# The last token group of a two-layer transformer kernel: first experts in two halves, and an unread TensorE product behind each piece

## The chip, the cores and the metric

The kernel runs on one core of a Trainium2 chip. The metric is the device time of one execution in microseconds (us); less is better. Five engines matter here: TensorE (PE in the profile, its weight loads PEld), VectorE (DVE), ScalarE (ACT), GpSimd (POOL) and SyncE (SP, which here issues the plain DMAs). Each engine takes its instructions from its own queue, strictly in order, and waits at an instruction until what it needs has been signalled.

## The reference: what is computed

One sequence of T = 2048 tokens of C = 128 features goes through two layers. Cut to what matters:

```python
x = x + attn0(layernorm(x))     # 16 heads of 64, softmax over all 2048 keys, and x again as residual
x = x + ffn0(layernorm(x))      # 16 experts; a token's weights are non-zero for 4 of them, out of 2 of 4 groups
x = x + attn1(layernorm(x))     # 8 heads; each token sees 64 local keys and 32 chosen ones
x = x + ffn1(layernorm(x))      # a shared expert of 256, and 2 of 8 experts fixed by the token's number
# attn1: I = sum_h iw[h] * relu(q_i[h] @ k_i.T); own 64 keys first, future ones out; top 96 by I
```

`attn1` needs, for every token, an index score against every earlier token, the 32 best of them, and their rows of keys and values.

## The kernel before, in words

**Tiles and groups.** Tokens lie in 16 tiles of 128 (one token to a partition) and 4 groups of 4 tiles. The main loop in `run` (L422) does layer 0's attention for all groups. Beside it, `advance` takes pieces of the later stages of a group whose attention is finished: `follow(g)` (L588) chains three Python generators, `experts0` (L599), `attention1` (L725) and `experts1` (L1055), and each `yield` hands back an estimated cost. When the attention ends, the last group (tiles 12 to 15) is left and nothing runs beside it: L502 to L505 close the attention's pools, set `self.alone` and run through `follow(3)`. I call this stretch the tail.

**The order of the work.** The code is traced in program order; a scheduler then puts each engine's instructions in an order by that priority and by its own model of when operands are ready. At run time each engine follows that list. An instruction passed to `keep_in_program_order` is pinned behind everything traced before it on its engine. In the tail a product takes its PSUM bank by `x()` (L138) from a cycle through all eight banks, `all_banks` (L120).

**`experts0`.** Layer norm (`layernorm`, L66), transposes (`transposed`, L145), then gating: a product `pg`, a sigmoid and comparisons that rank groups and experts (`below`, L637), weights `we`, and their transpose `ptw`. Every token goes through all 16 experts, with weight zero where it isn't routed. `hidden` (L710) is two products `p1b` and `p3b` of 512 columns (4 tiles of tokens) on PE, Tanh and Identity on ACT (L718, L719) and two DVE operations (L721, L722); then four products `py` (L702) and four DVE operations of 128x128 (L705) add the result to the residual `xr`. In the tail `ahead` = 4 experts' `hidden` are issued ahead. The weights `wb` come by SP, 192 KB an expert.

**`attention1`.** First, for 4 tiles together, layer norm and the products of keys and index queries (`pk`, `pm`, `ptk`: L733 to L781; I call it prepare), with a table of key rows written to DRAM. Then, tile by tile:
- `index_scores(n)` (L792): products `pi` (L802), Relu on ACT (L807), and DVE sums into the scores `v` (L804, L808), 64 + 128n wide, here 1600 to 1984.
- `choose(n)` (L824): four rounds of MAX8, FIND_INDEX8 and MATCH_REPLACE8 over `v` on DVE (L835, L837, L840), a transpose of the indices `ixT` (L842), and 32 indirect gathers of key rows into `kv` on POOL (L853), pinned in program order.
- `queries(n)` (L866): `pq`, softplus on ACT (L86 to L88: Abs, Exp, Ln), a rotation on DVE (L97 to L104), transposes `ptq` (L905).
- `attend(n)` (L913): rotation of the gathered rows on DVE (pinned), transposes `ptr`, scores `pl` (L942 adds a mask by a bf16 product of `identb` with `smask`, 416 columns), maxima and Exp (L962, L966), transposes `pte` (L983), `po`, and sixteen products `pj` (L1012) added to `xr` (L1013).

`beside(k, first, other)` takes k pieces of `other` behind each piece of `first`. The tail's order (L1031 to L1042) is: index 12, choose 12, index 13, choose 13; index 14 beside queries 12, choose 14 beside attend 12; the same with 15 and 13; then queries 14, attend 14, queries 15, attend 15. `experts1` follows.

Of the kernel before, what the change touches and what calls it, by code (L numbers as in the profile page):

```python
# [8 lines left out]
F32 = mybir.dt.float32  # L9
# [8 lines left out]
P = 128  # L18
# [88 lines left out]
class Program:  # L107
# [3 lines left out]
    def __init__(self, ctx, tc, a, out):  # L111
        self.ctx, self.tc, self.nc, self.a, self.out = ctx, tc, tc.nc, a, out
        nc = self.nc
        self.cp = ctx.enter_context(tc.tile_pool(name="const", bufs=1))
        self.dp = ctx.enter_context(tc.tile_pool(name="dram", bufs=1, space=DRAM))
        self.ps_s = ctx.enter_context(tc.tile_pool(name="ps", bufs=5, space=PSUM))
        self.ps_o = ctx.enter_context(tc.tile_pool(name="po", bufs=1, space=PSUM))
        self.ps_x = ctx.enter_context(tc.tile_pool(name="px", bufs=2, space=PSUM))
        s, o, x = (self.ps_s, "ps"), (self.ps_o, "po"), (self.ps_x, "x")
        self.all_banks = itertools.cycle((s, x, s, o, s, x, s, s))  # L120
        self.alone = False
# [22 lines left out]

    def transposed(self, src, dst, name):  # L145

        pt = self.x(name)
        for j in range(4):
            self.nc.tensor.transpose(pt[:, j, :], src[:, j, :], self.ident)
        self.nc.scalar.copy(dst, pt.rearrange("p a b -> p (a b)"))  # L150
# [271 lines left out]
    def run(self):  # L422
# [81 lines left out]
        for _ in self.follow(3):  # L504
            pass  # L505
# [82 lines left out]
    def follow(self, g):  # L588

        for stage in (self.experts0, self.attention1, self.experts1):  # L590
            with ExitStack() as sc:
                yield from stage(sc, g)
# [6 lines left out]
    def experts0(self, sc, g):  # L599
        nc, w, xr = self.nc, self.w, self.xr[g]  # L600
        sm = sc.enter_context(self.tc.tile_pool(name="b_sm", bufs=1, side="right"))

        ahead = 4 if self.alone else 0
        hp = sc.enter_context(self.tc.tile_pool(name="b_h", bufs=2 + ahead, side="right"))
        wp = sc.enter_context(self.tc.tile_pool(name="b_w", bufs=4 + ahead, side="right"))
        wx = [self.weights(wp, e, f"wb{g}_{e}") for e in range(2 + ahead)]
        xn = sm.tile([P, 4, C], F32, tag="xn", name=f"xn1_{g}")
        layernorm(nc, sm, xr, xn, "ln1")
        yield 5.0
        xT = sm.tile([P, 512], F32, tag="xT", name=f"xT1_{g}")  # L610
# [14 lines left out]
        pg = self.x(f"pg{g}", [P, 4, NE0])  # L625
        for j in range(4):
            nc.tensor.matmul(pg[:, j, :], xT[:, j * P : j * P + P], w["wg"], start=True, stop=True)
        s = sm.tile([P, 4, NE0], F32, tag="s", name=f"gs{g}")
# [8 lines left out]
        def below(v, n, first, k, tag):  # L637

            shape = [P, 4, n, n]
# [4 lines left out]
            ff = bcast(first.rearrange("p a b -> p (a b)"), 1, 4)  # L644
# [3 lines left out]
            rank = sm.tile([P, 4, n], F32, tag="rank" + tag, name=f"rank{tag}{g}")  # L648
# [4 lines left out]
        gm = sm.tile([P, 4, NG0], F32, tag="gm", name=f"gm{g}")  # L653
# [4 lines left out]
        goff = sm.tile([P, 4, NG0], F32, tag="goff", name=f"goff{g}")  # L658
        nc.vector.tensor_scalar(goff, gsel, 1.0, None, ALU.subtract)
        ms = sm.tile([P, 4, NE0], F32, tag="ms", name=f"ms{g}")  # L660
# [7 lines left out]
        we = sm.tile([P, 4, 32], F32, tag="we", name=f"we{g}")  # L668
        wh = sm.tile([P, 4, NE0], F32, tag="wh", name=f"wh{g}")
        nc.vector.memset(we, 0.0)  # L670
        nc.vector.tensor_tensor(we[:, :, 0:NE0], s, esel, ALU.mult)
        ws = sm.tile([P, 4], F32, tag="ws", name=f"ws{g}")
        wr = sm.tile([P, 4], F32, tag="wr", name=f"wr{g}")
# [6 lines left out]

        pt = self.x(f"ptw{g}", [P, P])
        nc.tensor.transpose(pt, we.rearrange("p a b -> p (a b)"), self.ident)
        wt = sm.tile([P, P], F32, tag="wt", name=f"wt{g}")
        nc.scalar.copy(wt, pt)
        yield 1.0
        pb = self.x(f"pb2_{g}")
        nc.tensor.matmul(pb.rearrange("p a b -> p (a b)"), wt, w["b2"], start=True, stop=True)
# [4 lines left out]
        for e in range(NE0 + 1):  # L692
            if e + ahead < NE0:
                if e + ahead + 2 < NE0:
                    wx.append(self.weights(wp, e + ahead + 2, f"wb{g}_{e + ahead + 2}"))
                hidden(e + ahead)
                yield 2.0
            if e > 0:
                h = hs.pop(e - 1)
                py = self.x(f"py{g}_{e}")  # L700
                for j in range(4):
                    nc.tensor.matmul(py[:, j, :], h[:, j * P : j * P + P], wx[e - 1][:, 2, :], start=True, stop=True)  # L702
                yield 1.0
                for j in range(4):
                    nc.vector.scalar_tensor_tensor(  # L705
                        xr[:, j, :], py[:, j, :], wh[:, j, e - 1 : e], xr[:, j, :], ALU.mult, ALU.add
                    )
                yield 1.0

    def hidden(self, pool, wx, xT, b1, hb1, b3, name):  # L710

        nc = self.nc
        p1, p3 = self.x("p1" + name, [P, 512]), self.x("p3" + name, [P, 512])
        nc.tensor.matmul(p1, wx[:, 0, :], xT, start=True, stop=True)  # L714
        nc.tensor.matmul(p3, wx[:, 1, :], xT, start=True, stop=True)  # L715
        th = pool.tile([P, 512], F32, tag="th", name="th" + name)
        z = pool.tile([P, 512], F32, tag="z", name="z" + name)
        nc.scalar.activation(th, p1, AF.Tanh, scale=0.5, bias=hb1)  # L718
        nc.scalar.activation(z, p1, AF.Identity, bias=b1)  # L719
        h = pool.tile([P, 512], F32, tag="h", name="h" + name)  # L720
        nc.vector.scalar_tensor_tensor(h, th, 1.0, z, ALU.add, ALU.mult)  # L721
        nc.vector.scalar_tensor_tensor(h, p3, b3, h, ALU.add, ALU.mult)  # L722
        return h

    def attention1(self, sc, g):  # L725
# [7 lines left out]
        cols = slice(512 * g, 512 * g + 512)  # L733
# [4 lines left out]
        with ExitStack() as prep:  # L738
            pp = prep.enter_context(tc.tile_pool(name="c_prep", bufs=1, side="right"))
            xn = pp.tile([P, 4, C], F32, tag="xn", name=f"xn2_{g}")  # L740
            layernorm(nc, pp, xr, xn, "ln2")
            yield 5.0
            xT = pp.tile([P, 512], F32, tag="xT", name=f"xT2_{g}")
            self.transposed(xn, xT, f"pt2_{g}")
# [3 lines left out]
            pk = self.x(f"pk{g}", [P, 4, 64])  # L748
            for j in range(4):
                nc.tensor.matmul(pk[:, j, :], xT[:, j * P : j * P + P], w["wck"], start=True, stop=True)  # L750
            kg = pp.tile([P, 4, 64], F32, tag="kg", name=f"kg{g}")
            nc.scalar.copy(kg[:, :, 0:32], pk[:, :, 0:32])
            softplus(nc, pp, kg[:, :, 32:64], pk[:, :, 32:64], self.one, "spk")
            nc.sync.dma_start(table.rearrange("(n p) d -> p n d", p=P)[:, 4 * g : 4 * g + 4, :], kg)
            yield 3.0
            for i, (dst, wt) in enumerate(
                ((kiT[:, cols], w["iwk"]), (qiT[0], w["iwq"][:, 0:128]), (qiT[1], w["iwq"][:, 128:256]), (cqT, w["wdq1"]))
            ):
                m = 64 if i == 3 else P
                pm = self.x(f"pm1_{g}_{i}", [P, 512])  # L760
# [7 lines left out]
            kl = pp.tile([P, 4, 2, 64], F32, tag="kl", name=f"kl{g}")  # L768
# [4 lines left out]
                cs[:, 0, 4 * g : 4 * g + 4, :], cs[:, 1, 4 * g : 4 * g + 4, :], "rk",  # L773
# [3 lines left out]
            pt = self.x(f"ptk{g}")  # L777
            for j in range(4):
# [3 lines left out]

        sm = sc.enter_context(tc.tile_pool(name="c_sm", bufs=2, side="right"))
# [8 lines left out]
        def index_scores(n):  # L792
# [4 lines left out]
            for lo in range(0, width, 512):  # L797
                hi = min(lo + 512, width)
                for h in range(4):
# [5 lines left out]
                    else:  # L805
                        rl = sm.tile([P, 512], F32, tag="rl", name=f"rl{n}_{lo}_{h}", bufs=6 if self.alone else 2)
# [59 lines left out]
        def queries(n):  # L866
# [33 lines left out]
            for i in range(2):  # L900
                t = sm.tile([P, P, NH1], F32, tag=f"qT{i}", name=f"qT{n}_{i}", bufs=3 if self.alone else 1)
# [344 lines left out]
```

## Time and profile before

| What | Number |
|---|---|
| median of 17 runs | 2806.57 us (2797.88 to 2815.09) |
| profiled execution, its own time | 2807.48 us |
| its span in the profile | 2805.7 us (1.78 us lie around it) |
| the tail, from `experts0`'s first layer norm to the end of the span | 2458.2 to 2805.7 us, 347.5 us |
| PE, DVE, ACT, POOL busy in the tail's twenty-us windows from 2460 | 219.89, 237.73, 129.77, 129.01 of 345.70 us |
| mean granted TensorE clock over the whole span | 0.94 |

The page gives one profiled execution. Its strips cut the span into 40 slices of 70.1 us; the tail is the last five. A line of the timeline has the start, the duration, the engine, the line of code and the operation (out<-in), shape, and in brackets the idle time before it with what ended it. A line of the windows view has, for a stretch of time, the busy us (and count) of each engine, the granted TensorE clock as a share of full speed, and the share of the DMA engines.

### The profile page before, as it was taken

What the parts mean: (1) busy time and instruction counts of PE and PEld (TensorE: products, weight loads), DVE (VectorE), ACT (ScalarE), POOL (GpSimd) and SP (SyncE); (2) the same over time, 40 slices, a digit from 0 to 9 for tenths busy, and PEclk for the clock granted to TensorE, in tenths of its full rate; (3) what the DMA queues carried; (4) which work ended last, traced back from release to release, by engine and by line L of the source; (5) the groups of instructions that cost most, each with busy time, mean ns of one, the idle gap of its engine ahead of it and who ended that gap; (6) DMA issues with size and microseconds to landing.
All of it is one profiled execution on the core that took longest, in us unless ns stands there. A gap on an engine that the chain in (4) does not pass through costs nothing. (4 is left out here: it accounts for less than half of the span.)

```text
span 2805.7 us, 39304 instructions
## 1 busy us (share of the span) xinstructions
PE 2539.2 (90%) x13452; PEld 1172.6 (42%) x13452; DVE 1671.1 (60%) x4650; ACT 1790.4 (64%) x4192; POOL 671.2 (24%) x964
## 2 busy tenths in 40 slices
PE   6999999999979999999999999999989999975566
PEld 3344444434434444434334444444333444442344
DVE  7655554565664454566686455466587654278863
ACT  3777778866656776856666677756666676533343
POOL 2111110000166520000066520000045560001771
PEclk9999999999999999999999999999999999986566
DMA  4322221111111211111111111111111120100111
GB/s 132 89 60 61 57 61 46 44 44 49 30 40 45 52 39 55 44 40 46 34 42 42 40 48 52 42 48 44 28 41 37 38 49 16 63 23 12 26 26 38
DMA packets 98103, 127.79 MB, mean 46 GB/s; under 512 B 31344, under 2 KB 49776, under 8 KB 97904
## 3 DMA queue, kind: packets, MB, share of 16 engines
q1 hardware_dynamic: 81520, 108.48, 13.7%
q0 software_dynamic: 16384, 16.81, 2.9%
q8 instruction: 106, 1.74, 0.3%
q14 instruction: 93, 0.76, 0.1%
HBM read 115.26 MB, written 9.96 MB: 45 GB/s over the span
## 5 line engine op out<-in xcount | busy, mean ns | idle before, releaser
L340 ACT ACTIVATE neg<-neg,mx 128x512 f32<-128x512 f32 x1024 | 729.8, 714 | 314.1 <-DVE neg L329 305.2
L329 DVE TENSOR_SCALAR_CACHE_REDUCE neg<-pa 128x512 f32<-128x512 f32 x1024 | 658.0, 686 | 432.8 <-PE pa L323 428.0
L390 ACT ACTIVATE e<-pb 128x512 f32<-128x512 f32 x1024 | 550.7, 595 | 289.0 <-PE pb L386 273.8
L384 PE MATMUL pb<-q,kb 64*128 64x512 f32 x2048 | 637.6, 626 | 8.9 <-DVE t_q L302 5.1
L323 PE MATMUL pa<-ka,q 64*128 64x512 f32 x2048 | 603.7, 628 | 20.0 <-ACT e L390 14.7
L853 POOL DMA_INDIRECT kv<-table,ixT x512 | 504.6, 986 | 424.3 <-DVE v L804 266.6
L399 PE MATMUL po<-e,ckv 128*64 128x512 f32 x2048 | 510.0, 611 | 0.0
L323 PEld LDWEIGHTS pa<-ka,q 64*128 64x128 f32 x2048 | 247.4, 192 | 226.4 <-issue 104.1
L303 POOL TENSOR_TENSOR q<-t_q 128x512 f32<-128x512 f32 x32 | 40.7, 1272 | 1209.5 <-DVE t_q L302 1117.0
L384 PEld LDWEIGHTS pb<-q,kb 64*128 64x128 f32 x2048 | 225.6, 189 | 207.8 <-issue 104.2
L386 PE MATMUL pb<-mrow,onesb 64*128 64x512 bf16 x1024 | 253.9, 383 | 7.8 <-ACT mrow L375 7.8
L399 PEld LDWEIGHTS po<-e,ckv 128*64 128x64 f32 x2048 | 126.7, 137 | 300.9 <-issue 283.5
L340 ACT ACTIVATION_READ_ACCUMULATOR neg<-neg,mx 128x1 f32 x1024 | 192.2, 188 | 0.0
L802 PE MATMUL pi<-kiT,qiT 64*128 64x512 f32 (+4 forms) x320 | 112.0, 612 | 26.4 <-DVE v L804 14.7
L386 PEld LDWEIGHTS <-onesb 64*128 64x128 bf16 x1024 | 69.2, 95 | 127.3 <-issue 119.1
L418 DVE SCALAR_TENSOR_TENSOR xr<-pp,rs,xr 128x128 f32<-128x128 f32 x256 | 72.3, 344 | 84.0 <-PE pp L415 71.8
L850 POOL COPY at<-kv 128x1 f32<-128x1 f32 x378 | 79.4, 217 | 175.9 <-DMA kv<-table,ixT 170.7
L721 DVE SCALAR_TENSOR_TENSOR hb<-thb,zb 128x512 f32<-128x512 f32 x64 | 44.3, 692 | 113.2 <-ACT zb L719 113.1
L808 DVE SCALAR_TENSOR_TENSOR v<-rl,iw_sb,v 128x512 f32<-128x512 f32 (+4 forms) x120 | 76.6, 643 | 50.7 <-ACT rl L807 46.6
L966 ACT ACTIVATE e<-pl,mx 128x208 f32<-128x208 f32 x128 | 54.3, 429 | 81.8 <-DVE mx L963 80.0
L303 POOL TENSOR_TENSOR kst<-t_k 128x512 f32<-128x512 f32 x32 | 41.0, 1281 | 264.4 <-DVE t_k L302 168.8
L962 DVE TENSOR_REDUCE mx<-pl 128x2 f32<-128x416 f32 x64 | 37.7, 590 | 101.1 <-PE pl L956 100.6
(276 smaller groups left out, 2861.6 us busy)
## 6 DMA issues: line engine op xcount, KB each, us to landing
ka<-kd SPq DMA_DIRECT2D x128, 256.0 KB
kb<-kd SPq DMA_DIRECT2D x128, 256.0 KB
wb<-in_wx SPq DMA_DIRECT2D x64, 192.0 KB
kd<-kst SPq DMA_DIRECT2D x32, 256.0 KB
kv<-table,ixT POOLq DMA_INDIRECT x512, 2.5
wd<-in_wx SPq DMA_DIRECT2D x40, 192.0 KB
csk<-in_cs SPq DMA_DIRECT2D x4, 512.0 KB
csq<-in_cs SPq DMA_DIRECT2D x4, 512.0 KB
```

The source lines that it names most:

```text
L303: nc.gpsimd.tensor_tensor(dst, t[:, 0, :], t[:, 1, :], ALU.add)
L323: nc.tensor.matmul(ps[h], q[rows, qt * P : qt * P + P], k[rows, :], start=True, stop=True)
L329: nc.vector.tensor_scalar(t, ps[h], -1.0, None, ALU.mult, ALU.min, accum_out=mx[at])
L340: nc.scalar.activation(t, t, AF.Exp, bias=mx[at], scale=-1.0, accum_out=su[at])
L384: nc.tensor.matmul(ps[h], k[rows, c], q[rows, :], start=True, stop=False)
L386: nc.tensor.matmul(ps[h], self.onesb[rows, :], mrow[rows, :], start=False, stop=True)
L390: nc.scalar.activation(e[:, h, :], ps[h], AF.Exp)
L399: nc.tensor.matmul(self.pos[u][cols, :], self.ckv[:, kb, :], e[:, h, :], start=(kb == 0), stop=(kb == NT - 1))
L802: nc.tensor.matmul(pi[:, : hi - lo], qiT[h // 2][rows, q], kiT[rows, lo:hi], start=True, stop=True)
L808: nc.vector.scalar_tensor_tensor(v[:, lo:hi], rl[:, : hi - lo], w["iw"][:, h : h + 1], v[:, lo:hi], ALU.mult, ALU.add)
L850: tc.keep_in_program_order(nc.gpsimd.tensor_copy(at[:, i : i + 1], slot))
L853: nc.gpsimd.indirect_dma_start(out=kv[:, 2 * (g % 16) + g // 16, :], out_offset=None, in_=table[0 : P * (n + 1), :], in_offset=bass.Indire ...
```

## The change

Three things change, all of them in the tail only.

**The filler.** A new method issues a product `spare<-identb,smask` of 128x416 in bf16, the form of L942, into the one `po` bank, which nobody reads. It is pinned in program order on PE. One is issued behind each piece of `follow(3)` that yields a cost other than zero: 325 of them, each a weight load and a product. `all_banks` then cycles through the other seven banks.

**Halves.** `experts0` takes a first tile and a number of tiles. In the tail `follow` does tiles 12 and 13 (products of 256 columns, pools on the other side of SBUF), then `attention1` prepares tiles 12 and 13. What is left, `rest()`, is `experts0` and prepare for tiles 14 and 15; two of its pieces stand behind each piece of index 12, choose 12, index 13, choose 13. Then index 14 beside queries 12 and the rest as before. The 16 experts' weights are loaded twice.

**Buffers.** `rl` has 4 buffers in place of 6, `qT` 2 in place of 3.

The diff, cut to its core (`4`, `512` and `P * 4` become `nt` and `P * nt` throughout `experts0`, `hidden` and prepare):

```diff
-        s, o, x = (self.ps_s, "ps"), (self.ps_o, "po"), (self.ps_x, "x")
-        self.all_banks = itertools.cycle((s, x, s, o, s, x, s, s))
+        s, x = (self.ps_s, "ps"), (self.ps_x, "x")
+        self.all_banks = itertools.cycle((s, x, s, s, x, s, s))
...
+    def filler(self):
+        if self.spare is None:
+            self.spare = self.ps_o.tile([P, 2 * NK], F32, tag="po", name="spare")
+        self.tc.keep_in_program_order(
+            self.nc.tensor.matmul(
+                self.spare, self.identb, self.smask[:, 0].rearrange("p a b -> p (a b)"), start=True, stop=True
+            )
+        )
...
-        for _ in self.follow(3):
-            pass
+        for us in self.follow(3):
+            if us:
+                self.filler()
...
-        for stage in (self.experts0, self.attention1, self.experts1):
+        with ExitStack() as sc:
+            yield from self.experts0(sc, g, 0, 2 if self.alone else 4)
+        for stage in (self.attention1, self.experts1):
...
-    def experts0(self, sc, g):
-        nc, w, xr = self.nc, self.w, self.xr[g]
+    def experts0(self, sc, g, t0, nt):
+        nc, w, xr = self.nc, self.w, self.xr[g][:, t0 : t0 + nt, :]
+        side, g = "left" if self.alone else "right", f"{g}_{t0}"
...
-        rl = sm.tile([P, 512], F32, tag="rl", name=f"rl{n}_{lo}_{h}", bufs=6 if self.alone else 2)
+        rl = sm.tile([P, 512], F32, tag="rl", name=f"rl{n}_{lo}_{h}", bufs=4 if self.alone else 2)
...
-            for m in range(n, n + 4):
-                if m < n + 2:
-                    yield from index_scores(m)
-                    yield from choose(m)
-                else:
-                    yield from beside(1, index_scores(m), queries(m - 2))
-                    yield from beside(3, choose(m), attend(m - 2))
-            for m in range(n + 2, n + 4):
+            def rest():
+                with ExitStack() as sb:
+                    yield from self.experts0(sb, g, 2, 2)
+                with ExitStack() as prep:
+                    yield from prepare(prep, 2, 2)
+
+            first = itertools.chain(*(f(m) for m in (n, n + 1) for f in (index_scores, choose)))
+            yield from beside(2, first, rest())
+            for m in (n + 2, n + 3):
+                yield from beside(1, index_scores(m), queries(m - 2))
+                yield from beside(3, choose(m), attend(m - 2))
+            for m in (n + 2, n + 3):
                 yield from queries(m)
                 yield from attend(m)
             return
```

More of the change, by code (lines that the diff above doesn't have):

```diff
@@ L118, in __init__ @@
         self.ps_x = ctx.enter_context(tc.tile_pool(name="px", bufs=2, space=PSUM))
-        s, o, x = (self.ps_s, "ps"), (self.ps_o, "po"), (self.ps_x, "x")
-        self.all_banks = itertools.cycle((s, x, s, o, s, x, s, s))
-        self.alone = False
+        s, x = (self.ps_s, "ps"), (self.ps_x, "x")
+        self.all_banks = itertools.cycle((s, x, s, s, x, s, s))
+        self.alone, self.spare = False, None
         self.ident = self.cp.tile([P, P], F32, tag="ident", name="ident")
@@ L143, in x @@
         return pool.tile(list(shape), dtype, tag=tag, name=name)
+    def filler(self):
[6 more added lines that the diff above has]
+        )
     def transposed(self, src, dst, name):
-        pt = self.x(name)
-        for j in range(4):
+        n = src.shape[1]
+        pt = self.x(name, [P, n, P])
+        for j in range(n):
             self.nc.tensor.transpose(pt[:, j, :], src[:, j, :], self.ident)
@@ L597, in weights @@
         return t
-    def experts0(self, sc, g):
-        nc, w, xr = self.nc, self.w, self.xr[g]
-        sm = sc.enter_context(self.tc.tile_pool(name="b_sm", bufs=1, side="right"))
+    def experts0(self, sc, g, t0, nt):
+        nc, w, xr = self.nc, self.w, self.xr[g][:, t0 : t0 + nt, :]
+        side, g = "left" if self.alone else "right", f"{g}_{t0}"
+        sm = sc.enter_context(self.tc.tile_pool(name="b_sm", bufs=1, side=side))
         ahead = 4 if self.alone else 0
-        hp = sc.enter_context(self.tc.tile_pool(name="b_h", bufs=2 + ahead, side="right"))
-        wp = sc.enter_context(self.tc.tile_pool(name="b_w", bufs=4 + ahead, side="right"))
+        hp = sc.enter_context(self.tc.tile_pool(name="b_h", bufs=2 + ahead, side=side))
+        wp = sc.enter_context(self.tc.tile_pool(name="b_w", bufs=4 + ahead, side=side))
         wx = [self.weights(wp, e, f"wb{g}_{e}") for e in range(2 + ahead)]
-        xn = sm.tile([P, 4, C], F32, tag="xn", name=f"xn1_{g}")
+        xn = sm.tile([P, nt, C], F32, tag="xn", name=f"xn1_{g}")
         layernorm(nc, sm, xr, xn, "ln1")
         yield 5.0
-        xT = sm.tile([P, 512], F32, tag="xT", name=f"xT1_{g}")
+        xT = sm.tile([P, P * nt], F32, tag="xT", name=f"xT1_{g}")
         self.transposed(xn, xT, f"pt1_{g}")
@@ L621, in experts0 @@
             hidden(e)
-        pg = self.x(f"pg{g}", [P, 4, NE0])
-        for j in range(4):
+        pg = self.x(f"pg{g}", [P, nt, NE0])
+        for j in range(nt):
             nc.tensor.matmul(pg[:, j, :], xT[:, j * P : j * P + P], w["wg"], start=True, stop=True)
-        s = sm.tile([P, 4, NE0], F32, tag="s", name=f"gs{g}")
+        s = sm.tile([P, nt, NE0], F32, tag="s", name=f"gs{g}")
         nc.vector.tensor_scalar(s, pg, -87.0, None, ALU.max)
@@ L637, in below @@
         def below(v, n, first, k, tag):
-            shape = [P, 4, n, n]
+            shape = [P, nt, n, n]
             gt = sm.tile(shape, F32, tag="gt", name=f"gt{tag}{g}")
@@ L643, in below @@
             nc.vector.tensor_tensor(eq, bcast(v, 2, n), bcast(v, 3, n), ALU.is_equal)
-            ff = bcast(first.rearrange("p a b -> p (a b)"), 1, 4)
+            ff = bcast(first.rearrange("p a b -> p (a b)"), 1, nt)
             e2 = eq.rearrange("p t a b -> p t (a b)")
@@ L647, in below @@
             nc.vector.tensor_tensor(gt, gt, eq, ALU.add)
-            rank = sm.tile([P, 4, n], F32, tag="rank" + tag, name=f"rank{tag}{g}")
+            rank = sm.tile([P, nt, n], F32, tag="rank" + tag, name=f"rank{tag}{g}")
             nc.vector.tensor_reduce(rank, gt, axis=AX.X, op=ALU.add)
@@ L651, in below @@
             return rank
-        gm = sm.tile([P, 4, NG0], F32, tag="gm", name=f"gm{g}")
+        gm = sm.tile([P, nt, NG0], F32, tag="gm", name=f"gm{g}")
         sg = s.rearrange("p t (g e) -> p t g e", g=NG0)
@@ L657, in experts0 @@
         yield 3.0
-        goff = sm.tile([P, 4, NG0], F32, tag="goff", name=f"goff{g}")
+        goff = sm.tile([P, nt, NG0], F32, tag="goff", name=f"goff{g}")
         nc.vector.tensor_scalar(goff, gsel, 1.0, None, ALU.subtract)
-        ms = sm.tile([P, 4, NE0], F32, tag="ms", name=f"ms{g}")
+        ms = sm.tile([P, nt, NE0], F32, tag="ms", name=f"ms{g}")
         msg = ms.rearrange("p t (g e) -> p t g e", g=NG0)
@@ L665, in experts0 @@
         yield 7.0
-        we = sm.tile([P, 4, 32], F32, tag="we", name=f"we{g}")
-        wh = sm.tile([P, 4, NE0], F32, tag="wh", name=f"wh{g}")
+        we = sm.tile([P, nt, 32], F32, tag="we", name=f"we{g}")
+        wh = sm.tile([P, nt, NE0], F32, tag="wh", name=f"wh{g}")
         nc.vector.memset(we, 0.0)
         nc.vector.tensor_tensor(we[:, :, 0:NE0], s, esel, ALU.mult)
-        ws = sm.tile([P, 4], F32, tag="ws", name=f"ws{g}")
-        wr = sm.tile([P, 4], F32, tag="wr", name=f"wr{g}")
+        ws = sm.tile([P, nt], F32, tag="ws", name=f"ws{g}")
+        wr = sm.tile([P, nt], F32, tag="wr", name=f"wr{g}")
         nc.vector.tensor_reduce(ws, we[:, :, 0:NE0], axis=AX.X, op=ALU.add)
@@ L679, in experts0 @@
         yield 2.0
+        rows = slice(0, 32 * nt)
         pt = self.x(f"ptw{g}", [P, P])
-        nc.tensor.transpose(pt, we.rearrange("p a b -> p (a b)"), self.ident)
+        nc.tensor.transpose(pt[rows], we.rearrange("p a b -> p (a b)"), self.ident)
         wt = sm.tile([P, P], F32, tag="wt", name=f"wt{g}")
-        nc.scalar.copy(wt, pt)
+        nc.scalar.copy(wt[rows], pt[rows])
         yield 1.0
-        pb = self.x(f"pb2_{g}")
-        nc.tensor.matmul(pb.rearrange("p a b -> p (a b)"), wt, w["b2"], start=True, stop=True)
+        pb = self.x(f"pb2_{g}", [P, nt, P])
+        nc.tensor.matmul(pb.rearrange("p a b -> p (a b)"), wt[rows], w["b2"][rows, 0 : P * nt], start=True, stop=True)
         nc.vector.tensor_tensor(xr, xr, pb, ALU.add)
@@ L699, in experts0 @@
                 h = hs.pop(e - 1)
-                py = self.x(f"py{g}_{e}")
-                for j in range(4):
+                py = self.x(f"py{g}_{e}", [P, nt, P])
+                for j in range(nt):
                     nc.tensor.matmul(py[:, j, :], h[:, j * P : j * P + P], wx[e - 1][:, 2, :], start=True, stop=True)
                 yield 1.0
-                for j in range(4):
+                for j in range(nt):
                     nc.vector.scalar_tensor_tensor(
@@ L712, in hidden @@
         nc = self.nc
-        p1, p3 = self.x("p1" + name, [P, 512]), self.x("p3" + name, [P, 512])
+        n = xT.shape[1]
+        p1, p3 = self.x("p1" + name, [P, n]), self.x("p3" + name, [P, n])
         nc.tensor.matmul(p1, wx[:, 0, :], xT, start=True, stop=True)
         nc.tensor.matmul(p3, wx[:, 1, :], xT, start=True, stop=True)
-        th = pool.tile([P, 512], F32, tag="th", name="th" + name)
-        z = pool.tile([P, 512], F32, tag="z", name="z" + name)
+        th = pool.tile([P, n], F32, tag="th", name="th" + name)
+        z = pool.tile([P, n], F32, tag="z", name="z" + name)
         nc.scalar.activation(th, p1, AF.Tanh, scale=0.5, bias=hb1)
         nc.scalar.activation(z, p1, AF.Identity, bias=b1)
-        h = pool.tile([P, 512], F32, tag="h", name="h" + name)
+        h = pool.tile([P, n], F32, tag="h", name="h" + name)
         nc.vector.scalar_tensor_tensor(h, th, 1.0, z, ALU.add, ALU.mult)
@@ L732, in attention1, with prepare @@
         st = sc.enter_context(tc.tile_pool(name="c_st", bufs=1, side="right"))
-        cols = slice(512 * g, 512 * g + 512)
         cqT = st.tile([64, 512], F32, tag="cqT", name=f"cqT1_{g}")
         qiT = [st.tile([P, 512], F32, tag=f"qiT{i}", name=f"qiT{g}_{i}") for i in range(2)]
-        with ExitStack() as prep:
+        def prepare(prep, t0, nt):
+            cols = slice(512 * g + P * t0, 512 * g + P * (t0 + nt))
+            part = slice(P * t0, P * (t0 + nt))
             pp = prep.enter_context(tc.tile_pool(name="c_prep", bufs=1, side="right"))
-            xn = pp.tile([P, 4, C], F32, tag="xn", name=f"xn2_{g}")
-            layernorm(nc, pp, xr, xn, "ln2")
+            xn = pp.tile([P, nt, C], F32, tag="xn", name=f"xn2_{g}_{t0}")
+            layernorm(nc, pp, xr[:, t0 : t0 + nt, :], xn, "ln2")
@@ L742, in attention1 @@
             yield 5.0
-            xT = pp.tile([P, 512], F32, tag="xT", name=f"xT2_{g}")
-            self.transposed(xn, xT, f"pt2_{g}")
+            xT = pp.tile([P, P * nt], F32, tag="xT", name=f"xT2_{g}_{t0}")
+            self.transposed(xn, xT, f"pt2_{g}_{t0}")
             yield 2.0
-            pk = self.x(f"pk{g}", [P, 4, 64])
-            for j in range(4):
+            pk = self.x(f"pk{g}_{t0}", [P, nt, 64])
+            for j in range(nt):
                 nc.tensor.matmul(pk[:, j, :], xT[:, j * P : j * P + P], w["wck"], start=True, stop=True)
-            kg = pp.tile([P, 4, 64], F32, tag="kg", name=f"kg{g}")
+            kg = pp.tile([P, nt, 64], F32, tag="kg", name=f"kg{g}_{t0}")
@@ L752, in attention1 @@
             nc.scalar.copy(kg[:, :, 0:32], pk[:, :, 0:32])
             softplus(nc, pp, kg[:, :, 32:64], pk[:, :, 32:64], self.one, "spk")
-            nc.sync.dma_start(table.rearrange("(n p) d -> p n d", p=P)[:, 4 * g : 4 * g + 4, :], kg)
+            nc.sync.dma_start(table.rearrange("(n p) d -> p n d", p=P)[:, 4 * g + t0 : 4 * g + t0 + nt, :], kg)
             yield 3.0
             for i, (dst, wt) in enumerate(
-                ((kiT[:, cols], w["iwk"]), (qiT[0], w["iwq"][:, 0:128]), (qiT[1], w["iwq"][:, 128:256]), (cqT, w["wdq1"]))
+                ((kiT[:, cols], w["iwk"]), (qiT[0][:, part], w["iwq"][:, 0:128]), (qiT[1][:, part], w["iwq"][:, 128:256]), (cqT[:, part], w["wdq1"]))
@@ L758, in attention1 @@
             ):
                 m = 64 if i == 3 else P
-                pm = self.x(f"pm1_{g}_{i}", [P, 512])
+                pm = self.x(f"pm1_{g}_{t0}_{i}", [P, P * nt])
                 nc.tensor.matmul(pm[:m, :], wt, xT, start=True, stop=True)
@@ L767, in attention1 @@
                 yield 1.0
-            kl = pp.tile([P, 4, 2, 64], F32, tag="kl", name=f"kl{g}")
+            kl = pp.tile([P, nt, 2, 64], F32, tag="kl", name=f"kl{g}_{t0}")
             nc.vector.tensor_copy(kl[:, :, 0, 0:32], kg[:, :, 0:32])
@@ L772, in attention1 @@
                 kg[:, :, 32:64].rearrange("p n (a b) -> p n a b", a=2),
-                cs[:, 0, 4 * g : 4 * g + 4, :], cs[:, 1, 4 * g : 4 * g + 4, :], "rk",
+                cs[:, 0, 4 * g + t0 : 4 * g + t0 + nt, :], cs[:, 1, 4 * g + t0 : 4 * g + t0 + nt, :], "rk",
             )
@@ L776, in attention1 @@
             yield 3.0
-            pt = self.x(f"ptk{g}")
-            for j in range(4):
+            pt = self.x(f"ptk{g}_{t0}", [P, nt, P])
+            for j in range(nt):
                 nc.tensor.transpose(pt[:, j, :], kl[:, j, :, :].rearrange("p a b -> p (a b)"), ident)
@@ L781, in attention1 @@
             yield 1.0
+        with ExitStack() as prep:
+            yield from prepare(prep, 0, 2 if self.alone else 4)
         sm = sc.enter_context(tc.tile_pool(name="c_sm", bufs=2, side="right"))
@@ L900, in queries @@
             for i in range(2):
-                t = sm.tile([P, P, NH1], F32, tag=f"qT{i}", name=f"qT{n}_{i}", bufs=3 if self.alone else 1)
+                t = sm.tile([P, P, NH1], F32, tag=f"qT{i}", name=f"qT{n}_{i}", bufs=2 if self.alone else 1)
                 for h in range(2):
@@ L1030, in attention1 @@
         if self.alone:
-            for m in range(n, n + 4):
-                if m < n + 2:
-                    yield from index_scores(m)
-                    yield from choose(m)
-                else:
-                    yield from beside(1, index_scores(m), queries(m - 2))
-                    yield from beside(3, choose(m), attend(m - 2))
-            for m in range(n + 2, n + 4):
+            def rest():
+                with ExitStack() as sb:
+                    yield from self.experts0(sb, g, 2, 2)
+                with ExitStack() as prep:
+                    yield from prepare(prep, 2, 2)
[5 more added lines that the diff above has]
+            for m in (n + 2, n + 3):
                 yield from queries(m)
```

## The prediction

> **What bounds the kernel now.** I read the page's strips first: where in the span does the picture change?
>
> ```profile
> PE   6999999999979999999999999999989999975566
> DVE  7655554565664454566686455466587654278863
> PEclk9999999999999999999999999999999999986566
> ```
>
> Up to slice 35 PE is at nine tenths and sets the pace; the change touches none of that. In the last five slices (the tail, from 2458.2 us) PE has 5 to 7 tenths, its clock 5 to 8, and DVE is at 7, 8 and 8 in three of them. So I cut the tail into stretches in the windows view (columns: stretch, its length, then busy us and count of PE, PEld, DVE, ACT, POOL, then granted clock, DMA share, GB/s):
>
> ```profile
> 2458.20:2525.40 67.20, 49.02 (x207) 29.94 (x207) 53.78 (x151) 22.55 (x36) 0.00 (x0) 0.85 0.08 24
> 2525.40:2541.10 15.70, 10.27 (x30) 5.56 (x32) 6.43 (x34) 4.67 (x10) 0.00 (x0) 0.67 0.05 10
> 2541.10:2553.30 12.20, 9.64 (x44) 4.29 (x44) 11.18 (x20) 7.48 (x16) 0.00 (x0) 0.86 0.14 20
> 2553.30:2579.70 26.40, 14.45 (x34) 4.77 (x30) 26.40 (x31) 7.39 (x17) 0.00 (x0) 0.65 0.02 3
> 2579.70:2609.00 29.30, 12.16 (x26) 5.64 (x26) 29.30 (x41) 6.47 (x11) 21.81 (x22) 0.50 0.12 24
> 2609.00:2655.80 46.80, 25.61 (x223) 16.66 (x222) 36.60 (x50) 15.23 (x42) 36.13 (x36) 0.56 0.13 26
> 2655.80:2708.80 53.00, 33.46 (x251) 19.53 (x250) 43.66 (x63) 23.54 (x58) 40.35 (x40) 0.68 0.12 25
> 2708.80:2749.80 41.00, 27.62 (x256) 21.41 (x255) 13.70 (x38) 20.98 (x56) 30.61 (x32) 0.66 0.14 26
> ```
>
> The rows are: first experts; prepare; index 12; then four stretches that end with the index transpose of tile 12, 13, 14 and 15; then the gathers of tile 15. From 2553.3 to 2609.0 DVE is busy for all 55.7 us, while PE stands at a clock of 0.65 and 0.50: there nothing but DVE matters. What sets the end, from the timeline:
>
> ```profile
> 2708.80 0.21 DVE L842 STREAM_TRANSPOSE ixT<-ix 128x32 uint32<-128x32 uint32 x1
> 2709.75 0.94 POOL L853 DMA_INDIRECT kv<-table,ixT  x1 [1.71 <-issue]
> 2748.97 0.94 POOL L853 DMA_INDIRECT kv<-table,ixT  x1 [0.30 <-issue]
> 2749.82 0.69 DVE L97 TENSOR_TENSOR w<-kv,cs 128x512 f32<-128x512 f32 x1 [1.44 <-DMA kv<-table,ixT]
> 2775.74 0.29 DVE L1013 TENSOR_TENSOR xr<-xr,pj 128x128 f32<-128x128 f32 x1 [12.52 <-PE pj L1012]
> ```
>
> When DVE finishes choose 15 (2708.8, call it T15), 32 gathers run for 41 us, attend 15 takes 26.2 us, and `experts1` and the last transfer 29.7 us. Everything before 2708.8 is one DVE queue of 250.6 us: 207.4 of work (the DVE column: 53.8 + 6.4 + 11.2 + 26.4 + 29.3 + 36.6 + 43.7) and 43.2 of idle. So **T15 decides, and DVE decides T15.** The POOL gathers are nearly as tight: back to back from 2580.8 to the end. A second chain (queries 14, attend 14, queries 15) ends at 2748.4, 1.4 us before the gathers.
>
> **The change part by part**, as a shift against the same point before.
>
> *First experts by halves.* Before, the steady expert takes 2.61 us: p1 and p3 0.86 each, py 0.89, so PE-bound at full clock. With 256 columns and two tiles PE has 0.43 + 0.43 + 0.44 = 1.30; DVE 2 x 0.42 (the 256-wide DVE rows) + 2 x 0.26 = 1.36. Three pieces yield per expert, so three fillers join on PE. A filler is the mask product of L942:
>
> ```profile
> 2755.99 0.35 PE L942 MATMUL pl<-smask_b,identb 128*128 128x416 bf16 x1
> 2756.27 0.67 PE L950 MATMUL pl<-kT,qT 64*128 64x80 f32 x4
> ```
>
> The next product starts 0.28 later, so a filler holds PE 0.28 us here; at half clock (2638.05 to 2638.51) 0.46. PE then has 1.30 + 0.84 = 2.14 an expert: fillers, not DVE, bound it. Twelve steady experts go from 31.3 to 25.7 us; the start (layer norm, four hiddens, gating, whose five 1024-wide operations of 1.22 halve) from 36 to about 28.5. First half: 54 us for 67, **-13**. Without fillers it would be -22. Weights come later, behind the attention's pools, but six transfers fit into layer norm and transposes.
>
> *Prepare for two tiles*: its 10.4 us from `xn` to the first score sum is a round trip through PE and ACT, not width: **-2**. Index 12 starts 15 earlier, at 2526.
>
> *The second half beside index 12 and choose 12.* DVE had 11.2 of 12.2 and 26.4 of 26.4 busy there, so there's no room: each operation is paid. Second-half work on DVE: gating about 8.5, 16 x 0.84 hiddens, 32 x 0.26 sums, layer norms of small 0.2 us steps about 8. Index 12 takes some 12 + 13.5 (gating, four hiddens, the first sums) + 4.5 (the gating's round trip through PE and ACT, 3.3 before, with an extra activation table load, 1.28 in its row) = 30 us: choose 12 starts at 2556. Its eleven operations of 1.82 plus some eight experts make 30: the transpose of tile 12 falls at 2586, **+6**. Index 13 (which the scheduler had put inside choose 12), the rest of the second half and choose 13 (eleven of 1.96) make 40 for 29.3: tile 13 at 2626, **+17**.
>
> *Prepare for tiles 14 and 15.* In the changed order on DVE the tail of this layer norm, its `xn` and the key rotation stand behind the transpose of tile 13, and the first sum of index 14 behind them. Before, index 14 stood inside choose 13 and was done 5.9 us after it. Now the round trip (10.4 before; shorter products, but a table load and fillers, eight of them just ahead of the first `pi14`) lies bare: 12.5, then index 14 with queries 12 about 17 (16.1 in the like stretch 2655.8 to 2671.9). That is 29.5 for 5.9: +23.6. Back comes the wait of attend 12 for its gathers:
>
> ```profile
> 2626.25 0.69 DVE L97 TENSOR_TENSOR w<-kv,cs 128x512 f32<-128x512 f32 x1 [5.32 <-DMA kv<-table,ixT]
> ```
>
> These are long landed now, and choose 14 goes from 40.9 to 34: -7. Tile 14 at 2689, **+34**. Index 15 and choose 15 stay at about 53: T15 **+34**.
>
> *After T15.* Gathers 41, as before. The second chain gets some 37 fillers and four table loads (Ln and Exp take turns on ACT: the tail has 13 loads for 3). Half the fillers fall into PE's waits, so about +5 + 3 of loads, against PE work of 27.6 us at a clock of 0.66, which may gain 4. It had 1.4 in hand: **+3**. Attend 15 and `experts1`: 24 and 8 fillers, half of them bare, +4, less the same from the clock: **0**.
>
> *Smaller edits.* Seven banks for eight, `rl` 4 for 6, `qT` 2 for 3: in the tail `x()` serves PE results that ACT or DVE read at once; waits for banks show as DVE v L804 and ACT rl L807 in front of `pi`, off the bound. I take 0; ends: -1 and +5 (the 4.3 us that L804 waits for PE, doubled). The extra 3.1 MB of weights run at a DMA share of 0.17 at most: 0. SP's cl loads stay behind them: nothing waits.
>
> **Sum**: -13 -2 +21 (to +6) +11 +17 (to +34) +3 = **+37**; 2807.5 + 37 = 2844.5, I say **2845**. The profiled execution lies 0.9 above the median, so either base serves.
>
> *Check from the other side.* DVE has 207 us before T15; halves add small steps that don't shrink (layer norms 6, gating 2, hiddens 5, rest 1): 221. Idle: 22 in the first half (54 less 32), 7 prepare, 5 gating, 12 second prepare, 18 for the rest: 64. 2458.2 + 221 + 64 = 2743 = T15 + 34.
>
> *Bounds of the fillers.* 325 of them cost from -15 (all in waits; PE's 27.6 us at 0.66 behind T15 lose 9, and some 13 at 0.5 in attend 15 lose 6) to +50 (0.46 each, a third bare). I take 0.28 where PE bounds or is in a round trip: some 70 bare, about +20 in the sum (9 in the first half, 3 ahead of index 14, 4 to 5 each in the second chain and attend 15), and -8 for the clock in the last two. What idle time does to the clock, the trace shows: PE idles 10.16 us before `ptw`; its clock is 0.50 from 2480 to 2488 and 1.00 from 2492 to 2496. But a filler waits for nothing. Those behind choose's pieces run in a bunch as soon as PE comes to them, up to eight in a row, and PE then stands still until DVE is done, as before.
>
> [...]
>
> **Rivals.**
> 1. *Faster.* DVE's idle shrinks: with 221 us of work T15 comes before 2708.8 only if less than 29.6 us of idle are left (64 in my sum). For it: PE is idle a third of the tail. It needs the second half to fill waits, but the stretches that it's put into have none. With 15 us of idle, T15 is -15: 2793.
> 2. *Only tile 12's shift counts.* Gathers run back to back, 41 a tile; if prepare hides and DVE is never late after tile 12, the end moves by +6 to +17: 2813 to 2825. Against it: DVE's order behind tile 13.
> 3. *Fillers dear*: clock low, 0.46 each, and some 85 to 110 bare for 70: 18 to 30 more: 2863 to 2875.
> 4. *It doesn't do what it says*: the clock stays as it is in choose. Within my forecast; without its gains of 8 the end is 2853.
>
> **How the numbers follow.** The forecast with rival 4: 0.62 (2828 to 2863). Rival 2: 0.12. Rival 3: 0.10. Faster: 0.11. Rival 1 half done, within 0.2% (5.6 us, about what a measurement of this kernel can tell): 0.05. The range leaves out rival 1, no change and rival 3's far end: 2811 to 2870. Slower 0.84.
>
> **What would show it.** Index transposes of tiles 12, 13, 14, 15 at 2586, 2626, 2689, 2743; DVE idle some 10 us between tile 13's and the first sum of index 14; steady first experts at 2.1 us each; clock near 0.5 still in choose. Wrong if T15 comes before 2709 or fillers hold PE far from 0.28.

## The result, and the profile after

The changed kernel takes 2851.55 us (median of 8 runs, 2846.91 to 2860.47), the kernel before 2807.68 (46 runs): a ratio of 1.0159 (95% interval 1.0144 to 1.0174), or +44.6 us. Forecast were 2845 and a range of 2811 to 2870. The profiled execution of the changed kernel took 2857.3 us, 5.75 above the median.

The attention ahead of the tail ends at another time in every execution (in these profiles between 2451.8 and 2471.1 us, in code that no kernel here touches). So I count from the tail's start, the first statistics of `experts0`: 2458.19 before, 2457.99 after. Shifts against before, in us, from the DVE timelines of one profile each. One profile is one execution: two kernels that differ only in edits that cost nothing (experiments 9 and 3) have tails of 355.6 and 369.7 us in theirs, so a few us in one column prove little by themselves.

| Point | before | forecast | after | halves alone | halves, covered |
|---|---|---|---|---|---|
| first score sum, index 12 | 82.9 | -15 | -18.9 | -28.8 | -26.7 |
| index transpose, tile 12 | 121.5 | +6 | +3.8 | -9.5 | -0.5 |
| tile 13 | 150.8 | +17 | +11.8 | +7.3 | +19.0 |
| tile 14 | 197.6 | +34 | +27.0 | +25.4 | +16.2 |
| tile 15 (T15) | 250.6 | +34 | +37.4 | +30.7 | +24.2 |
| rotation of tile 15's gathered rows | 291.6 | +37 | +47.2 | +37.6 | +31.0 |
| end of the span | 347.5 | +37 | +50.0 | +37.8 | +32.0 |

The windows view of the changed kernel, cut at the same points as before, with prepare and index 12 in one row, the second (index 14 to choose 14 begin at 2620.60, the last two rows are attend 15 and `experts1`):

```profile
2458.00:2508.80 50.80, 38.71 (x189) 30.01 (x189) 33.20 (x113) 15.58 (x36) 0.00 (x0) 0.80 0.16 49
2508.80:2554.80 46.00, 33.49 (x131) 18.38 (x132) 29.97 (x111) 17.02 (x42) 0.00 (x0) 0.81 0.17 48
2554.80:2583.30 28.50, 23.74 (x112) 14.05 (x110) 28.48 (x47) 7.99 (x19) 0.00 (x0) 1.00 0.14 42
2583.30:2620.60 37.30, 12.75 (x65) 6.25 (x64) 37.30 (x69) 4.73 (x10) 27.92 (x28) 0.70 0.13 24
2620.60:2682.60 62.00, 44.31 (x256) 23.53 (x256) 45.62 (x76) 30.49 (x69) 34.87 (x36) 0.79 0.13 24
2682.60:2746.00 63.40, 48.05 (x328) 25.14 (x331) 45.67 (x64) 26.76 (x61) 32.66 (x32) 0.73 0.09 17
2746.00:2796.80 50.80, 36.79 (x367) 24.41 (x360) 14.22 (x39) 26.88 (x63) 31.51 (x32) 0.76 0.11 22
2796.80:2822.90 26.10, 22.71 (x247) 15.34 (x246) 7.61 (x19) 15.40 (x40) 0.00 (x0) 0.88 0.01 2
2822.90:2855.50 32.60, 21.02 (x91) 14.55 (x91) 10.81 (x35) 6.09 (x8) 0.00 (x0) 0.67 0.22 69
```

Read the third and fourth rows first: in choose 12 and choose 13 DVE is still busy for every microsecond, now for 65.8 us where it was 55.7, while the granted clock stands at 1.00 and 0.70. The clock has come up from 0.65 and 0.50, and nothing there could use it but the second half's own work. Then rows five and six: 125.4 us for the 99.8 before, with 34.1 us of DVE idle in them for 19.5. The time is lost there and in row seven, 50.8 us for 41.0.

Row seven, from the DVE and POOL timelines of the changed kernel:

```profile
2745.98 0.21 DVE L865 STREAM_TRANSPOSE ixT<-ix 128x32 uint32<-128x32 uint32 x1
2751.25 0.29 DVE L1036 TENSOR_TENSOR xr<-xr,pj 128x128 f32<-128x128 f32 x1 [5.06 <-PE pj L1035]
2786.95 0.94 POOL L876 DMA_INDIRECT kv<-table,ixT  x1 [0.30 <-issue]
2796.76 0.69 DVE L97 TENSOR_TENSOR w<-kv,cs 128x512 f32<-128x512 f32 x1 [1.79 <-PE ptq L928]
```

The last gather of tile 15 is issued 41.0 us after T15, 40.2 before. But the rotation of its rows starts 9.8 us later, released by PE (`ptq`, from queries 15): the second chain now ends well behind the gathers.

### The profile page after: what moved, and what is told of

It reads as the page before. It is cut to its first block, busy times and chain, and to the rows that moved or that the text cites. A ratio compares the mean times of both kernels' runs of the same rounds, so it can differ in the third digit from the quotient of the medians.

```text
span 2855.5 us, 40322 instructions
## 1 busy us (share of the span) xinstructions
PE 2605.5 (91%) x13853; PEld 1211.4 (42%) x13853; DVE 1685.4 (59%) x4746; ACT 1810.9 (63%) x4247; POOL 670.7 (23%) x964
## 5 line engine op out<-in xcount | busy, mean ns | idle before, releaser
L396 PE MATMUL pb<-q,kb 64*128 64x512 f32 x2048 | 646.7, 633 | 8.3 <-DVE t_q L314 5.2
L335 PE MATMUL pa<-ka,q 64*128 64x512 f32 x2048 | 597.8, 620 | 19.4 <-ACT e L402 13.3
L825 PE MATMUL pi<-kiT,qiT 64*128 64x512 f32 (+4 forms) x320 | 105.3, 577 | 12.0 <-ACT mrow L387 3.1
L741 DVE SCALAR_TENSOR_TENSOR hb<-thb,zb 128x512 f32<-128x512 f32 (+1 forms) x80 | 46.6, 584 | 116.6 <-ACT zb L739 116.6
L151 PE MATMUL spare<-smask_b,identb 128*128 128x416 bf16 x326 | 103.8, 388 | 0.0
```

What stands on the lines that cost most here:

```text
L151: self.nc.tensor.matmul(self.spare, self.identb, self.smask[:, 0].rearrange("p a b -> p (a b)"), start=True, stop=True)
L335: nc.tensor.matmul(ps[h], q[rows, qt * P : qt * P + P], k[rows, :], start=True, stop=True)
L396: nc.tensor.matmul(ps[h], k[rows, c], q[rows, :], start=True, stop=False)
L825: nc.tensor.matmul(pi[:, : hi - lo], qiT[h // 2][rows, q], kiT[rows, lo:hi], start=True, stop=True)
```

## The experiments

Theory 1: the split of the first experts is the loss, because DVE is full where the second half is put and the second prepare lies bare; the fillers add a little on PE. Rival A: the fillers are the loss. Rival B: the fillers pay by the clock, and the split costs more than the whole. Each kernel ran beside the kernel before on the same chip. Ratios are against that; "us" is the ratio's distance from 1 times 2807.68.

**1. Halves without fillers.**

```diff
         for us in self.follow(3):
-            if us:
-                self.filler()
+            pass
```

> The changed kernel without its 325 fillers, all else as it is (halves, seven banks, buffers). Theory 1 (the split is the loss, the fillers add a little): 10 to 16 us less than the changed kernel, so about 2838 to 2842; the steady expert of the first half falls from 1.84 to about 1.4 us, the index transposes of tiles 13 to 15 still come 8 to 30 us later than before. Rival A (the fillers are the loss): 2812 or less. Rival B (the fillers pay by the clock, the split costs more than the whole): 2855 or more.

Measured: 1.0137 (1.0095 to 1.0179), +38.5 us. The split is the loss, as theory 1 said: rival A is out. But taking the fillers away gave back some 6 us by the ratios, not 10 to 16, and the intervals overlap, so by this experiment alone rival B isn't excluded; experiment 2, where fillers without a split cost time, speaks against it. The profile shows where the gain goes. The steady expert falls from 1.84 to about 1.36 us, and the first score sum comes 9.9 us earlier, tile 12's transpose 13.3. Then most of it is given back, between the transposes of tiles 12 and 13 (windows view, halves alone, then after):

```profile
2572.00:2618.10 46.10, 20.73 (x52) 9.62 (x50) 38.14 (x70) 5.68 (x12) 30.39 (x32) 0.57 0.10 23
```

```profile
2583.30:2620.60 37.30, 12.75 (x65) 6.25 (x64) 37.30 (x69) 4.73 (x10) 27.92 (x28) 0.70 0.13 24
```

DVE has the same work (38.1 and 37.3), but without fillers it stands idle for 8 of 46.1 us, at a PE clock of 0.57: 4.6 of it waiting for PE (`pi`, `py`) and 3.3 for ACT's `rl`. With fillers it waits for neither. So here the fillers go with a fuller DVE, and of the 13.3 us by which they are behind at tile 12, 4.5 are left at tile 13. That the clock does it, and not the other order of the work, isn't shown.

**2. Fillers without halves**, on the kernel before, with seven banks.

> The kernel before with a filler behind each piece of the last group's stages, and seven banks; no halves. Theory 1: +8 to +14 us (0.17 us three times an expert on a PE that is the bound there, some in the chain behind the last choose, nothing where DVE is the bound): 2815 to 2822. Rival A (the fillers are the loss): +30 or more. Rival B (they pay by the clock): 2800 or less.

**6. The same, fillers behind the first experts' pieces only; 7. behind what follows the last choose only** (a flag `warm`, set for `experts0` alone or from queries 14 on):

```diff
-            if us:
+            if us and self.warm:
                 self.filler()
```

> The kernel before with fillers behind the pieces of the first experts only (about 50 of them), seven banks. Theory 1: PE is the bound of 12 steady experts, three fillers of 0.175 us each: 6 to 10 us, so 2813 to 2817. Rival B (a warm clock pays): 2806 or less.

> The kernel before with fillers behind the last choose only (queries 14 to the end, about 70), seven banks. Theory 1: the last choose doesn't move; the chain of queries 14, attend 14, queries 15, which the gathers only just cover, takes their place; attend 15 gains from the clock what the fillers cost: +3 to +8, 2810 to 2815. Rival B (the warm clock pays in the two chains behind the last choose): 2804 or less.

Measured: 1.0066 (1.0046 to 1.0085), 1.0064 (1.0043 to 1.0085) and 1.0044 (1.0026 to 1.0062): +18.5, +18.0, +12.4 us. All three lie above what I expected, because I had priced the seven banks at nothing; rival A, +30 or more, and rival B, a gain, are out. Against experiment 9 (the banks alone, +10.9) the fillers cost 7.6, 7.1 and 1.4 us, with intervals that overlap. What the profiles add is the place: in the first experts a steady expert of 512 columns rises from 2.61 to 3.14 us, by three fillers of 0.175, and the first score sum comes 8.5 and 7.4 us later than in 9. Behind the last choose no cost can be told from noise. In choose 13 the clock is 0.56 for 0.50 and the stretch 29.7 for 29.3 us, from the windows view of fillers alone:

```profile
2592.90:2622.60 29.70, 17.37 (x36) 5.96 (x35) 29.70 (x41) 6.79 (x12) 21.81 (x22) 0.56 0.10 24
```

**3. The smaller edits alone** (seven banks, `rl` 4, `qT` 2), **9. seven banks alone, 10. the two buffers alone**, on the kernel before:

```diff
-        self.all_banks = itertools.cycle((s, x, s, o, s, x, s, s))
+        self.all_banks = itertools.cycle((s, x, s, s, x, s, s))
```

> The kernel before with seven banks, four rl and two qT buffers; no fillers, no halves. Theory 1: within 3 us of before. Rival (banks carry part of the loss, shown as waits of DVE L804 for PE): +5 or more.

> The kernel before with seven banks in the cycle and nothing else. Theory 1, added to after the earlier runs (with seven banks the first index product of tile 15, and the queries of tile 13, stand behind the output products of attend 12 on PE, and VectorE waits): +3 to +9, so 2811 to 2817, and the stretch between the index transposes of tiles 14 and 15 is 57 us or more for 53. Rival (the stretch is long because of the clock in that run, or of the fewer rl and qT buffers): within 2 us of before.

> The kernel before with four rl and two qT buffers and eight banks. Theory 1: within 2 us of before, the stretch between the transposes of tiles 14 and 15 about 53. Rival (the buffers make that stretch long): +3 or more.

Measured: 1.0015 (0.9993 to 1.0036), 1.0039 (1.0019 to 1.0058) and 0.9993 (0.9980 to 1.0006). The buffers cost nothing. The banks do, on this kernel: +10.9 us (5 to 16) in 9, a little more than the 3 to 9 that I expected there; experiment 3, which has them too, gave +4.2 (-2 to 10), so the size is uncertain. In the profiles of 2, 3, 6, 7 and 9 the stretch between the transposes of tiles 14 and 15 is 59.9 to 66.0 us; before and in 10 it is 53. PE's order shows it, in the timelines of before and of seven banks:

```profile
2652.61 0.69 PE L802 MATMUL pi<-kiT,qiT 64*128 64x512 f32 x1
2652.61 0.69 PE L877 MATMUL pq<-wq,cqT 64*128 64x512 f32 x1
...
2654.49 2.05 PE L1012 MATMUL pj<-wvo,lt 32*128 32x128 f32 x16 [0.76 <-ACT lt L1005]
```

```profile
2664.10 1.98 PE L802 MATMUL pi<-kiT,qiT 64*128 64x512 f32 x4
2666.15 2.05 PE L1012 MATMUL pj<-wvo,lt 32*128 32x128 f32 x16
2668.13 2.04 PE L802 MATMUL pi<-kiT,qiT 64*128 64x512 f32 x2
2669.96 1.91 PE L877 MATMUL pq<-wq,cqT 64*128 64x512 f32 x2
```

With eight banks the queries of tile 13 (`pq`) and tile 15's first index product stand ahead of `pj`, attend 12's output; with seven they stand behind it (the `pi` at 2668.13 is the one that tile 15's first sum, DVE L804 at 2670.20, waits for). The first sum of tile 15 and all of queries 13 come later, and choose 15 starts 25.1 us after tile 14's transpose instead of 16.1.

**4. One activation table**, in the changed kernel:

```diff
+                tc.keep_in_program_order(nc.scalar.preload_act_table_set("natural_log_exp_and_others"))
                 with ExitStack() as prep:
                     yield from prepare(prep, 2, 2)
```

> The changed kernel with one activation table, that with Exp and Ln, set again ahead of prepare for tiles 14 and 15: eight fewer table loads of 1.28 us. Theory 1: five of the eight stand on the path (second prepare, queries 12 or 13, queries 14, the Exp of attend 14, queries 15): 4 to 7 us less than the changed kernel, 2845 to 2848. Rival (they lie in ACT's idle time): no change.

**5. The second prepare covered**, on the halves without fillers, **and 8. with the table of 4**:

```diff
-            yield from beside(2, first, rest())
+            yield from beside(3, first, rest())
```

> The halves without fillers, with three pieces of the second half behind each piece of index 12 to choose 13 in place of two, so that prepare for tiles 14 and 15 comes ahead of choose 13 on VectorE and index 14 stands inside choose 13 again. Theory 1 (the uncovered round trip of that prepare is a good third of the split's loss): 10 to 15 us less than the halves alone, 2834 to 2840; tile 14's index transpose 10 or more us earlier against tile 12's. Rival C (only the added VectorE work and the second chain count, where it stands doesn't matter): within 4 us of the halves alone, 2846 to 2854.

> As the covered halves without fillers, and the activation table with Exp and Ln set again ahead of the second prepare. Theory 1: 3 to 7 us less than the covered halves, 2828 to 2836, still slower than the kernel before. Rival: no difference to the covered halves.

Measured: 4 gave 1.0134 (1.0103 to 1.0164), 5 gave 1.0099 (1.0080 to 1.0117), 8 gave 1.0108 (1.0085 to 1.0132). The table's gain on the changed kernel is about 7 us with intervals that overlap, and none shows in 8 against 5, where theory 1 failed: it stays open, and is small. Experiment 5 is clear of the changed kernel by its interval, and 10.7 us below the halves alone, as theory 1 had it; against these the intervals overlap at their edges. The same edit with eight banks (12 against 11, below) gains 14.6 us, with intervals apart. The profiles show what it covers. In the changed kernel (DVE, then ACT):

```profile
2620.60 0.21 DVE L865 STREAM_TRANSPOSE ixT<-ix 128x32 uint32<-128x32 uint32 x1
...
2624.56 0.20 DVE L790 COPY kl<-kg 128x64 f32<-128x64 f32 x1 [2.44 <-ACT kg L773]
2626.64 0.23 DVE L89 SCALAR_TENSOR_TENSOR kg<-pk,spka 128x64 f32<-128x64 f32 x1 [1.88 <-ACT spka L88]
...
2631.28 0.75 DVE L827 TENSOR_SCALAR v<-pi,iw_sb 128x512 f32<-128x512 f32 x1 [3.43 <-PE pi L825]
```

```profile
2624.96 1.28 ACT L88 ACT_TABLE_LOAD   x1
```

and with three pieces for one:

```profile
2630.94 0.21 DVE L864 STREAM_TRANSPOSE ixT<-ix 128x32 uint32<-128x32 uint32 x1
...
2638.06 2.10 DVE L857 MAX8 m<-v 128x8 f32<-128x1856 f32 x1
```

From tile 13's transpose to choose 14 it is 7.1 us in the covered kernel, against 32.1 in the changed one, 30.1 in the halves alone and 5.9 before. Part of it moves: tile 13 comes 11.7 us later than in the halves alone, and the round trip's waits (2.41 us for `kg`, 1.88 for `spka`) now lie inside index 13.

**11. and 12. The halves, and the covered halves, with eight banks**, no fillers.

> The halves without fillers, with eight banks. Theory 1: 4 to 9 us less than with seven, 2837 to 2842. Rival: no difference, 2844 or more.

> The covered halves (three pieces of the second half for one), no fillers, with eight banks. Theory 1: 4 to 9 us less than with seven, 2827 to 2832, what is left being the VectorE work that the split adds and its round trips: still 20 us slower than before. Rival: no difference.

Measured: 1.0140 (1.0121 to 1.0160) and 1.0088 (1.0067 to 1.0109), against 1.0137 and 1.0099 with seven. Theory 1 failed in 11, and the 3 us in 12 don't clear the noise: where the work is split, the eighth bank is worth nothing that shows. The best of all the halves, 12, is still +24.7 us. Its profile says what is left: T15 comes 22.9 us later than before, 11.1 of it added DVE work (218.5 us for 207.4) and 11.8 added idle time. No kernel of this study beat the one before.

## Why the prediction was right, point by point

- *T15 decides, and DVE decides T15.* Held for the larger part: T15 +34 was forecast, +37.4 measured, of +50.0 in that profile; the rest arose behind T15. The first six rows of the windows after hold 220.2 us of DVE work (forecast 221) in 288.0, so 67.8 of idle (forecast 64).
- *First experts by halves, -13.* Measured -16.4 (67.2 to 50.8). The term of the fillers was too dear: I took 0.28 us from the row of L942, where the next product uses 64 rows. In the first experts the next uses 128 rows and starts after 0.18 (PE timeline, after):

```profile
2494.17 0.34 PE L151 MATMUL spare<-smask_b,identb 128*128 128x416 bf16 x1
2494.35 0.61 PE L721 MATMUL py<-wb,hb 128*128 128x128 f32 x4
2494.79 0.52 PE L151 MATMUL spare<-smask_b,identb 128*128 128x416 bf16 x2
2495.14 0.59 PE L734 MATMUL p1b<-xT,wb 128*128 128x256 f32 x2
```

  The two fillers behind `py` take 0.35 us from start to start (2494.79 to 2495.14), 0.175 each. So three are 0.53, not 0.84, an expert takes 1.84, not 2.14 (3.6 us over twelve), and it is still PE that bounds it. Ahead of a product of 64 rows a filler still holds PE 0.28 in this trace (2689.90 to 2690.18, where `pq` follows). Without fillers I had said -22; the halves alone reach the first statistics of prepare 24.5 us earlier than before.
- *The second half must be paid on DVE.* Held, at +3.8 and +11.8 for +6 and +17. In choose 12 and choose 13 DVE was busy throughout; in prepare and index 12, ahead of them, for 30.0 of 46.0 us.
- *The second prepare lies bare, +23.6.* Held: choose 14 starts 32.1 us after tile 13's transpose for 5.9, +26.2, and experiment 5 brings the halves from 30.1 to 7.1. Choose 14 with attend 12 fell to 29.9 us, not 34.
- *Index 15 and choose 15 stay at about 53.* Wrong: 63.4. It is the largest miss. Choose 15 itself kept its 37; the 10 us lie ahead of it, where DVE waits for PE (`pi`, `pj`). The same place is long in every kernel with seven banks (59.9 to 66.0, or 58.3 in the halves alone); the banks alone bring choose 15 to 25.1 us after tile 14's transpose, the changed kernel to 26.1, from 16.1. With the split, eight banks shorten the stretch to 56.9 (from 58.3) and, covered, to 55.8 (from 61.0). So bank order is a part, and the split's and the fillers' shares weren't separated. I had put the seven banks at nothing, at most +5 with the other small edits, without looking at PE's order: +10.9 on the kernel before.
- *The second chain, +3.* Wrong in size: +9.8, and the 1.4 us that I took it to have in hand weren't there. The wait that the view puts to the DMA before is as long as the one ahead of tile 14's rotation, and in experiment 10, whose tail takes 347.4 us, the same wait is put to PE (before, tile 14; then experiment 10, tile 15):

```profile
2716.83 0.69 DVE L97 TENSOR_TENSOR w<-kv,cs 128x512 f32<-128x512 f32 x1 [1.44 <-PE ptq L905]
```

```profile
2756.06 0.69 DVE L97 TENSOR_TENSOR w<-kv,cs 128x512 f32<-128x512 f32 x1 [1.44 <-PE ptq L905]
```

  So the second chain ended no earlier than the gathers before the change, too, and all that lengthens it shows. Of the 9.8 us, 8.2 are there at tile 14's rotation: attend 13's last sum comes 3.5 later, queries 14 behind it 4.3, its transposes 0.4. Three table loads (3.8 us) stand in the chain, but without them it shrinks by 1.7 (experiment 4) and 1.4 (8 against 5) only. The fillers aren't all of it: the halves alone have 47.9 us from T15 to tile 15's rotation, for 41.0 before. Nor is PE's order enough: `pq` of queries 14, at 2704.54 ahead of attend 13's `pj` (2708.50) before, runs behind it, at 2751.95 after 2749.16, but so it does in every kernel with seven banks, and with eight (experiment 11) it stands ahead again and the chain has 47.4.

  What the profiles do show is the clock: with no split and no fillers, T15 to tile 15's rotation takes 41.0 us at a granted clock of 0.66 (before) and 48.7 at 0.54 (experiment 3); from tile 14's rotation to tile 15's it is 33.0 and 38.5, and 29.9 in experiment 9. How the 9.8 divide stays open.
- *Attend 15 and `experts1`, 0.* Attend 15 took 26.1 us for 26.4 before, at a clock of 0.88 for 0.63: that fits clock and fillers cancelling, as said. `experts1` took 32.6 for 29.5, 3 us that I hadn't forecast.
- *Clock near 0.5 still in choose* (rival 4). Wrong: 1.00 and 0.70 in choose 12 and 13. The second half's products stand among the fillers there; without fillers it is 0.72 and 0.57. The fillers ran in bunches of up to seven in choose 12, two in choose 13 and four in choose 14 and 15; the bunch of eight ahead of index 14 came as forecast. The risen clock changed no sign: it kept DVE full at best, where the halves alone left it idle for 8 us.
- The errors offset each other in part: -7 at tile 14, +10 in index 15, +7 in the second chain, +3 in `experts1`. That 2845 came so near to 2851.55 is partly luck: T15 came close because two errors ahead of it nearly cancelled, the stretch behind it was mis-sized, and the profiled execution ended 13 us later than forecast where the median is 7 later.

Rival 2 is out (tile 12's shift is +3.8), rival 1 too (67.8 us of idle, where it needed less than 29.6). Rival 3 is out: where fillers bound PE, a filler is cheaper than I said (0.175 us for 0.28), not dearer.

## What to carry to other kernels

Before work is moved to cover waits, read the busy time of the engine that bounds the stretch it's moved into: where DVE is busy for 55.7 of 55.7 us, all that was moved there was paid, and fillers alone, with a clock of 0.69 on PE for 0.57, didn't shorten it (56.4 us). Splitting a stage in two also gave it a second round trip through the other engines, which needed cover of its own (choose 14 began 32.1 us after tile 13's transpose, and 7.1 once the round trip was covered): look in the compiled order for what stands behind it. And an edit that only takes a bank out of a cycle can reorder an engine's queue (+10.9 us in experiment 9); price it from the order of instructions, not from the wait rows.

## What the runs showed that I had not expected

A PE that was busy all the time wasn't always granted its full clock. In the profile of experiment 3 PE has work for all of 14 us, and the clock stays at 0.50 (windows view); with fillers alone it does so for 13:

```profile
2656.00:2670.00 14.00, 14.00 (x32) 7.47 (x32) 2.60 (x5) 3.72 (x11) 10.64 (x11) 0.50 0.11 26
```

```profile
2670.00:2683.00 13.00, 13.00 (x24) 3.29 (x22) 5.73 (x12) 3.43 (x8) 9.95 (x11) 0.50 0.11 26
```

In the first case it had been at 0.50 since 2608.8 at the latest (the mean of 2608.8 to 2655.2), in the second it fell from 1.00 (2665 to 2669) just behind `pj`. In the changed kernel the same products, in nearly the same order, ran at 1.00 (2682 to 2696). The products themselves say the same (fillers alone, then after):

```profile
2671.37 2.07 PE L814 MATMUL pi<-kiT,qiT 64*128 64x512 f32 x2
```

```profile
2688.84 1.12 PE L825 MATMUL pi<-kiT,qiT 64*128 64x512 f32 x2
```

These two stretches are 14 and 13 us of unbroken work by the profile's busy time, and the clock was 0.50 in both. What decides it, the kind of product or the moment, isn't settled here. The clock goes with some of the spread: of the twelve runs of experiment 9, the two fastest (2807.91 and 2808.08 us) had a mean clock of 0.941 and 0.942, the two slowest (2830.51 and 2835.34) of 0.932.
